# Pair bias with 8 stationary weights in four column strips, x loaded ahead of the pair, group statistics in whole-array steps

## The chip, the cores and the metric

The kernel runs on one core of one Trainium2 chip, with all data in 32-bit floating point. The metric is the device time of one execution in microseconds (us). PE is the matmul engine, PEld its loads of stationary weights, DVE the vector engine, ACT the scalar engine, POOL the GpSimd engine, and SP the engine whose queue issues most of the DMA transfers.

## The reference, cut to what matters

x has 128 rows s of 256 positions and 256 channels. Two layers follow one another, each of the form x + attention(groupnorm(x)), with 32 groups of 8 channels whose mean and variance are taken over all rows and positions.

```python
# layer 0: 8 heads of 32 channels
bias = einsum('nijz,zh->nhij', pair_repr, bias_proj)      # pair_repr: 256 x 256 x 128, bias_proj: 128 x 8
gate = sigmoid(xn @ gate_proj)
q, k, v = split(xn @ qkv_proj, 3)
sim = softmax(q k^T / sqrt(32)) + bias                    # the bias comes after the softmax
x = x + ((sim v) * gate) @ out_proj
# layer 1: 4 heads of 64 channels, keys within 16 positions of the query
q, k, v = split(xn @ w_in.T + b_in, 3)
x = x + softmax(mask(q k^T / sqrt(64))) v @ w_out.T + b_out
```

## The kernel before, in words

The program is written with named tiles in pools. A scheduler keeps each engine's instructions close to the written order and puts in the waits; a tile of a pool with n buffers is written again only when the use n tiles before is over. PSUM is shared by three pools: two banks for projections (`proj_bank`, taken in turn by everything that asks), four for scores (`sim_bank`), and one each of `avz` and `bv0`.

**Pair stage.** Eight chunks of x (32 positions per partition, `x_chunk`, L148) are loaded and their statistics taken with 32 `bn_stats` (L153), one per group. Sixteen chunks of the pair (`pair_chunk`, L181), each 32 values of i by 128 of j, go into a bias table `bias_sb` with j on the partitions. A chunk is transposed on PE four blocks at a time (L192), copied out of PSUM by ACT (L194), and then every transposed block of 128x128 is loaded as the stationary operand and multiplied with the 8 columns of `bias_w_sb` (L197). A last copy (L202) puts heads and i in order. The loop takes one chunk of x and one of the pair by turns (L207), so SP's queue has their loads (L151, L184) by turns, two buffers for each. After the loop `group_columns` (L110) makes mean and 1/std per channel: 32 `bn_aggr` on DVE (L113), then two small matmuls over partitions (L117, L130), a square root on ACT (L139) and a reciprocal (L141).

**Layer 0.** Each row s has two half steps, one per four heads. A half step makes scores of its four heads (L311), then some projections (in half 0: q and k of the next row and the transposes px of the row after; in half 1: v and the gate of the next row, and the output projection po of the row before), then `attend` for the half step before. The projections take the two proj banks in the fixed order q, k, px, v, gate, po. ACT makes the exponentials `ex` (L318) and copies q, k and v; DVE adds the two key tiles of `ex` (`both`, L321), since the denominator is a matmul of ones with that sum (L349). `attend` multiplies `ex` and the bias table with v in four column strips (L336, L343), and then:

```python
nc.scalar.activation(z, avz[:, 1, :], AF.Identity, accum_out=zsum[:, n : n + 1])   # L354
nc.vector.tensor_tensor(t, bv0, z, ALU.mult)                                       # L356
nc.vector.tensor_tensor(t, avz[:, 0, :], t, ALU.add)                               # L357
nc.vector.scalar_tensor_tensor(d, st[s]["e"][:, half, :], 1.0, z, ...)             # L359
nc.vector.reciprocal(d, d)                                                         # L360
nc.vector.tensor_tensor(st[s]["at"][:, half, :], t, d, ALU.mult)                   # L363
nc.vector.tensor_reduce(zmin[:, n : n + 1], z, axis=AX.X, op=ALU.min)              # L364
```

`finish` (L366) adds x to po (L374); every eighth row it stores the block and takes its statistics with 32 `bn_stats` (L379). After the last row `group_columns` runs again for layer 1, and the first loads of layer 1 (L414) wait for its last instruction.

**Layer 1** has one step per row, with masked exponentials multiplied on POOL (L455), z copied with its sum (L479), a reciprocal of 512 columns (L481), `at` (L483), the minimum (L485), and additions on DVE (L435, L495) and POOL (L496).

The minima and sums of z serve a test at the end (L519 to L530): if a denominator was outside a range of safe values, both layers are computed again with shifted exponentials. With these inputs that part isn't entered.

Of the kernel before, what the change touches and what calls it, by code (L numbers as in the profile page):

```python
# [9 lines left out]
F32 = mybir.dt.float32  # L10
AF = mybir.ActivationFunctionType
ALU = mybir.AluOpType
# [19 lines left out]
def conv_preact_kernel(  # L32
# [37 lines left out]
    eps = const.tile([P, 1], F32, name="eps")  # L70
    nc.gpsimd.memset(eps, EPS)

    bias_w_sb = const.tile([P, H0], F32, name="bias_w_sb")
    nc.scalar.dma_start(out=bias_w_sb, in_=bias_w)
    qkv_sb = const.tile([P, 2, 3 * C], F32, name="qkv_sb")
    nc.scalar.dma_start(out=qkv_sb, in_=qkv_w.rearrange("(t p) o -> p t o", p=P))
    gate_sb = const.tile([P, 2, C], F32, name="gate_sb")
# [29 lines left out]
    zsum = const.tile([P, 3 * S], F32, name="zsum")  # L107


    def group_columns(pool, stats, which):  # L110
        mv = pool.tile([P, G, 2], F32, name=f"mv{which}")
        for g in range(G):
            nc.vector.bn_aggr(out=mv[:, g, :], in_=stats[:, g, :, :].rearrange("p n s -> p (n s)"))  # L113
        means = pool.tile([P, G], F32, name=f"means{which}")
        nc.vector.tensor_copy(means, mv[:, :, 0])
        ps_m = proj_bank(f"ps_m{which}")
        nc.tensor.matmul(ps_m[:, 0, 0:G], lhsT=avg, rhs=means, start=True, stop=True)  # L117
        d = pool.tile([P, G], F32, name=f"d{which}")
        nc.vector.tensor_tensor(d, means, ps_m[:, 0, 0:G], ALU.subtract)
        v = pool.tile([P, G], F32, name=f"v{which}")  # L120
        nc.vector.tensor_tensor(v, d, d, ALU.mult)
        nc.vector.tensor_tensor(v, v, mv[:, :, 1], ALU.add)
        wide = pool.tile([P, 2, G, CG], F32, name=f"wide{which}")
        nc.vector.tensor_copy(wide[:, 0], means.unsqueeze(2).to_broadcast([P, G, CG]))
        nc.vector.tensor_copy(wide[:, 1], v.unsqueeze(2).to_broadcast([P, G, CG]))
        flat = wide.rearrange("p k g c -> p k (g c)")
        ps_c = proj_bank(f"ps_c{which}")
        for k in range(2):
            for half in range(2):
                nc.tensor.matmul(  # L130
                    ps_c[:, 0, 2 * k + half : 2 * k + half + 1],
                    lhsT=flat[:, k, half * P : (half + 1) * P],
                    rhs=avg[:, 0:1],
                    start=True, stop=True,
                )
        mean = const.tile([P, 2], F32, name=f"mean{which}")
        nc.vector.tensor_copy(mean, ps_c[:, 0, 0:2])
        std = pool.tile([P, 2], F32, name=f"std{which}")
        nc.scalar.activation(std, ps_c[:, 0, 2:4], AF.Sqrt, bias=eps)  # L139
        rstd = const.tile([P, 2], F32, name=f"rstd{which}")  # L140
        nc.vector.reciprocal(rstd, std)  # L141
        return mean, rstd
# [12 lines left out]

    with ExitStack() as early:
        xs_pool = early.enter_context(tc.tile_pool(name="xs", bufs=2))
        pr_pool = early.enter_context(tc.tile_pool(name="pr", bufs=2))
        st_pool = early.enter_context(tc.tile_pool(name="st", bufs=1))

        w_nat = st_pool.tile([P, 8, C], F32, name="w_nat")
        nc.scalar.dma_start(out=w_nat[:, 0:6, :], in_=w_in.rearrange("(t p) c -> p t c", p=P))
        nc.scalar.dma_start(out=w_nat[:, 6:8, :], in_=w_out.rearrange("(t p) c -> p t c", p=P))
        for o4 in range(2):
            for kt in range(2):
                pw = proj_bank(f"pw{o4}_{kt}").rearrange("p a b -> p (a b)")
                for j in range(4):
                    nc.tensor.transpose(
                        pw[:, j * P : (j + 1) * P], w_nat[:, 4 * o4 + j, kt * P : (kt + 1) * P], ident
                    )  # L170
                if o4 == 0:
                    nc.scalar.copy(w_in_t[:, kt, 0:512], pw)
                else:
                    nc.scalar.copy(w_in_t[:, kt, 512:768], pw[:, 0:256])
                    nc.scalar.copy(w_out_t[:, kt, :], pw[:, 256:512])

        stats = st_pool.tile([P, G, NX, 6], F32, name="stats0")
        IC = 32
        NPR = 2 * (R // IC)

        def pair_chunk(n):  # L181
            kt, ic = divmod(n, R // IC)
            pr = pr_pool.tile([P, IC, Z], F32, tag="pr", name=f"pr{n}")
            nc.sync.dma_start(  # L184
                out=pr,
                in_=pair[0, ic * IC : (ic + 1) * IC, kt * P : (kt + 1) * P, :].rearrange("i j z -> j i z"),
            )
            pb = proj_bank(f"pb{n}").rearrange("p a b -> p (a b)")
            for i4 in range(IC // 4):
                pz = sim_bank(f"pz{n}_{i4}").rearrange("p a b -> p (a b)")  # L190
                for i in range(4):
                    nc.tensor.transpose(pz[:, i * P : (i + 1) * P], pr[:, 4 * i4 + i, :], ident)  # L192
                prt = pr_pool.tile([P, 512], F32, tag="prt", name=f"prt{n}_{i4}", bufs=3)
                nc.scalar.copy(prt, pz)  # L194
                for i in range(4):
                    ii = 4 * i4 + i
                    nc.tensor.matmul(  # L197
                        pb[:, ii * H0 : (ii + 1) * H0],
                        lhsT=prt[:, i * P : (i + 1) * P], rhs=bias_w_sb,
                        start=True, stop=True,  # L200
                    )
            nc.scalar.copy(  # L202
                bias_sb[:, kt, :, ic * IC : (ic + 1) * IC],
                pb[:, 0 : IC * H0].rearrange("p (i h) -> p h i", h=H0),
            )

        for n in range(max(NX, NPR)):  # L207
            if n < NX:
                x_chunk(xs_pool, stats, x[0], n, "0_")
            if n < NPR:  # L210
                pair_chunk(n)
        mean0, rstd0 = group_columns(st_pool, stats, 0)


    XG = min(4, S)
# [40 lines left out]
    def rows(ap, s0, n):  # L256
        return ap[s0 : s0 + n].rearrange("s (t p) c -> p s t c", p=P)

    x1 = dram.tile([S, R, C], F32, name="x1")
    SG = min(8, S)  # L260

# [4 lines left out]
    with ExitStack() as lay:  # L266
        st1 = lay.enter_context(tc.tile_pool(name="st1", bufs=1))
        stats1 = st1.tile([P, G, S // SG, 6], F32, name="stats1")
        with ExitStack() as lay0:
# [11 lines left out]
            def piece(s, n):  # L281
# [6 lines left out]
                elif n in (1, 2):  # L288
                    w = "qk"[n - 1]
                    ps = by_channel(qkv_sb, (n - 1) * C, st[s]["xn"], f"p{w}{s}")  # L290
                    a = row.tile([P, 2, R], F32, tag=w, name=f"{w}{s}")
                    nc.scalar.copy(a, ps)
                    st[s][w] = a
                elif n == 3:
                    ps = by_token(st[s]["xn"], qkv_sb, 2 * C, f"pv{s}")
                    v = row.tile([P, 2, C], F32, tag="v", name=f"v{s}", bufs=3)
                    nc.scalar.copy(v, ps)
                    st[s]["v"] = v
                elif n == 4:
                    ps = by_channel(gate_sb, 0, st[s]["xn"], f"pg{s}")  # L300
                    e = row.tile([P, 2, R], F32, tag="e", name=f"e{s}", bufs=3)
                    nc.scalar.activation(e, ps, AF.Exp, scale=-1.0)
                    st[s]["e"] = e

            def scores(s, half):
# [11 lines left out]
                for j in range(4):  # L317
                    nc.scalar.activation(ex[:, j], sims[j], AF.Exp, scale=1.0 / math.sqrt(D0))  # L318
                both = att.tile([P, 4, R], F32, tag="both", name=f"both{s}_{half}")
                for j in range(0, 4, 2):  # L320
                    nc.vector.tensor_tensor(both[:, j : j + 2], ex[:, j : j + 2, 0, :], ex[:, j : j + 2, 1, :], ALU.add)  # L321
                hd[s, half] = (ex, both)

            def attend(s, half):
# [25 lines left out]
                        avz[ps, 1, :], lhsT=ones[:, 0:D0], rhs=both[:, j, :], start=True, stop=True  # L350
                    )
                z = att.tile([P, R], F32, tag="z", name=f"z{s}_{half}")
                n = 2 * s + half
                nc.scalar.activation(z, avz[:, 1, :], AF.Identity, accum_out=zsum[:, n : n + 1])  # L354
                t = att.tile([P, R], F32, tag="t", name=f"t{s}_{half}")
                nc.vector.tensor_tensor(t, bv0, z, ALU.mult)  # L356
                nc.vector.tensor_tensor(t, avz[:, 0, :], t, ALU.add)  # L357
# [3 lines left out]
                if half == 0:  # L361
                    st[s]["at"] = row.tile([P, 2, R], F32, tag="at", name=f"at{s}")
                nc.vector.tensor_tensor(st[s]["at"][:, half, :], t, d, ALU.mult)  # L363
                nc.vector.tensor_reduce(zmin[:, n : n + 1], z, axis=AX.X, op=ALU.min)  # L364

            def finish(s):  # L366
                if s < 0:
# [20 lines left out]
            for i in range(n_steps + 2):  # L388
# [10 lines left out]
                    finish(s - 1)  # L399
                if 0 <= i - 1 < n_steps:  # L400
                    attend(*divmod(i - 1, 2))
        mean1, rstd1 = group_columns(st1, stats1, 1)


    with ExitStack() as lay:
# [55 lines left out]
        def attend(s):  # L461
# [13 lines left out]
                                start=(kt == 0), stop=(kt == 1), skip_group_check=True,  # L475
                            )
            z = att.tile([P, 2, R], F32, tag="z", name=f"1z{s}")
            n = 2 * S + s
            nc.scalar.activation(z, zs, AF.Identity, accum_out=zsum[:, n : n + 1])  # L479
            rz = att.tile([P, 2, R], F32, tag="rz", name=f"1rz{s}")  # L480
            nc.vector.reciprocal(rz, z)  # L481
            at = row.tile([P, 2, R], F32, tag="at", name=f"1at{s}")
            nc.vector.tensor_tensor(at, av, rz, ALU.mult)  # L483
            st[s]["at"] = at
            nc.vector.tensor_reduce(zmin[:, n : n + 1], z, axis=AX.XY, op=ALU.min)  # L485

        def finish(s):
            if s < 0:
# [41 lines left out]
    with tc.If(sure < P):  # L530
        with ExitStack() as lay:
# [103 lines left out]
                again(0, s, x[0], x1, mean0, rstd0)  # L635
            for n in range(NX):
                x_chunk(two, stats2, x1, n, "2_")
            mean2, rstd2 = group_columns(one, stats2, 2)
            with tc.For_i(0, S, 1) as s:
                again(1, s, x1, out[0], mean2, rstd2)  # L640

# [24 lines left out]
```

## Time and profile before

| what | us |
|---|---|
| median of the 3 runs (3970.82 to 3972.38) | 3971.9 |
| the profiled execution, its own time | 3971.9 |
| its span, first to last instruction | 3970.1 |
| first transposes of the pair | 29.25 |
| first load of layer 0's rows issued | 348.3 |
| first transposes of layer 0 (px) | 354.3 |
| last addition of layer 0 (L374) | 2458.9 |
| first transposes of layer 1 | 2489.6 |

Busy shares of the span: PE 98%, PEld 77%, DVE 62%, ACT 37%, POOL 13%; mean granted PE clock 0.951.

How to read the profile: the page cuts the span into 40 slices of 99 us, one digit per slice, the busy share in tenths, and "PEclk" the share of the full clock that PE was granted. In the timeline a line has the start, the time in us from the first start to the last end of like instructions that follow each other, the engine, the line, the tiles as output<-inputs, shapes, the number of instructions and in brackets the idle time before with what ended it. A matmul of 32-bit data is two records. The records of matmuls overlap, so a PE that is busy all the time isn't a PE at its peak; where it matters the distance from one start to the next is given. In a group a line ends with the busy time of all, the mean duration of one in ns, and the idle time before.

### The profile page before, as it was taken

Reading aid. Unit: us, or ns where it says so; the run is one execution under the profiler, and the core shown is the slowest. Engines: PE = TensorE matmul, PEld = TensorE weight load, DVE = VectorE, ACT = ScalarE, POOL = GpSimd, SP = SyncE. Lnnn points to the kernel's source line nnn. Section 1 sums busy time; section 2 is a strip of 40 time slices with the busy share of each in tenths; the row PEclk is TensorE's granted clock in tenths of the full one; section 3 lists DMA queues with packets and bytes.
Section 4 is the critical chain, followed back from the end, with each engine's and each line's share of the span. In section 5 each row is a group of like instructions: output and inputs, shape, how many; then the busy total and the mean of one; then the engine's idle time right before and its main releaser. Section 6 shows DMA issues by size and latency. Waiting matters only on the chain. (4 is left out here: it accounts for less than half of the span.)

```text
span 3970.1 us, 75105 instructions
## 1 busy us (share of the span) xinstructions
PE 3877.4 (98%) x32294; PEld 3057.5 (77%) x32294; DVE 2457.1 (62%) x4181; ACT 1487.1 (37%) x3485; POOL 501.2 (13%) x270
## 2 busy tenths in 40 slices
PE   7999999999999999999999997999999999999998
PEld 7998777777777777777777774788888888888887
DVE  5402677767776777677766777456556555555655
ACT  2223444444444444444444442333333333333332
POOL 0000000000000000000000000233333333333333
PEclk6556999999999999999999998999999999999999
DMA  9631011101110111001110100111111111111111
GB/s 360 217 106 54 12 44 33 44 12 44 33 44 12 44 35 42 26 30 44 33 41 15 44 23 22 54 43 43 53 55 43 43 43 43 60 48 43 43 43 33
DMA packets 153826, 208.83 MB, mean 53 GB/s; under 512 B 2960, under 2 KB 135824, under 8 KB 152464
## 3 DMA queue, kind: packets, MB, share of 16 engines
q1 hardware_dynamic: 150656, 201.34, 15.8%
q8 instruction: 256, 4.19, 0.4%
q10 hardware_dynamic: 2832, 2.63, 0.2%
q14 instruction: 82, 0.67, 0.1%
HBM read 136.85 MB, written 67.11 MB: 51 GB/s over the span
## 5 line engine op out<-in xcount | busy, mean ns | idle before, releaser
L455 POOL TENSOR_TENSOR 1p<-1ex,seen 128x1152 f32<-128x1152 f32 x128 | 336.0, 2625 | 2758.9 <-ACT 1ex L453 2758.9
L481 DVE RECIPROCAL 1rz<-1z 128x512 f32<-128x512 f32 x128 | 429.2, 3353 | 246.9 <-ACT 1z L479 246.9
L318 ACT ACTIVATE ex<-sim 128x512 f32<-128x512 f32 x1024 | 528.7, 602 | 129.0 <-PE sim L311 129.0
L360 DVE RECIPROCAL d<-d 128x256 f32<-128x256 f32 x256 | 445.9, 1742 | 0.0
L356 DVE TENSOR_TENSOR t<-bv,z 128x256 f32<-128x256 f32 x256 | 108.1, 422 | 460.2 <-ACT z L354 460.2
L354 ACT ACTIVATE z<-avz 128x256 f32<-128x256 f32 x256 | 98.3, 384 | 750.4 <-PE avz L349 739.2
L479 ACT ACTIVATE 1z<-1zs 128x512 f32<-128x512 f32 x128 | 76.4, 597 | 729.0 <-issue 719.8
L321 DVE TENSOR_TENSOR both<-ex 128x512 f32<-128x512 f32 x512 | 329.1, 683 | 2.9 <-ACT ex L318 2.9
L311 PE MATMUL sim<-q,k 32*128 32x256 f32 x4096 | 293.3, 400 | 0.0
L336 PE MATMUL avz<-ex,v 128*32 128x256 f32 x4096 | 275.6, 386 | 10.5 <-DVE t L357 10.5
L343 PE MATMUL bv<-bias_sb,v 128*32 128x256 f32 x4096 | 269.6, 379 | 1.1 <-DVE t L356 1.1
L311 PEld LDWEIGHTS sim<-q,k 32*128 32x128 f32 x4096 | 184.9, 184 | 110.5 <-issue 104.9
L227 DVE TENSOR_SCALAR xn<-px,mean,rstd 128x256 f32<-128x256 f32 x512 | 253.8, 537 | 23.8 <-PE px L222 21.3
L250 PE MATMUL 1po<-w_out_t,1at 128*128 128x256 f32 x1024 | 256.9, 394 | 0.8 <-DVE 1at L483 0.8
L239 PE MATMUL p1q<-xn,w_in_t 128*128 128x256 f32 x1024 | 257.0, 394 | 0.6 <-DVE xn L227 0.6
L239 PE MATMUL pq<-xn,qkv_sb 128*128 128x256 f32 x1024 | 256.7, 394 | 0.8 <-DVE xn L227 0.7
L250 PE MATMUL pv<-qkv_sb,xn 128*128 128x256 f32 x1024 | 255.1, 392 | 0.0
L250 PE MATMUL po<-out_sb,at 128*128 128x256 f32 x1024 | 247.5, 382 | 6.5 <-DVE at L363 4.9
L496 POOL TENSOR_TENSOR 1o<-1o,yg 128x512 f32<-128x512 f32 x128 | 162.9, 1273 | 701.8 <-DVE 1o L495 699.2
L239 PE MATMUL p1k<-xn,w_in_t 128*128 128x256 f32 x1024 | 242.4, 380 | 0.0
L239 PE MATMUL pg<-xn,gate_sb 128*128 128x256 f32 x1024 | 241.9, 379 | 0.0
L250 PE MATMUL p1v<-w_in_t,xn 128*128 128x256 f32 x1024 | 241.9, 379 | 0.0
(91 smaller groups left out, 6314.6 us busy)
## 6 DMA issues: line engine op xcount, KB each, us to landing
xs<-in_x_dram SPq DMA_DIRECT2D x8, 4096.0 KB, 22.1
xg<-in_x_dram SPq DMA_DIRECT2D x32, 1024.0 KB, 7.5
x<-o SPq DMA_DIRECT2D x16, 2048.0 KB, 8.4
yg<-x SPq DMA_DIRECT2D x32, 1024.0 KB, 8.1
out_dram<-1o SPq DMA_DIRECT2D x32, 1024.0 KB, 5.3
qkv_sb<-in_L_conv_qkv_proj_dram ACTq DMA_DIRECT2D x1, 768.0 KB, 13.7
w_nat<-in_L_conv_w_in_dram ACTq DMA_DIRECT2D x1, 768.0 KB, 8.0
gate_sb<-in_L_conv_gate_proj_dram ACTq DMA_DIRECT2D x1, 256.0 KB, 14.0
```

The source lines that it names most:

```text
L227: nc.vector.tensor_scalar(xn[:, half, :], px[:, half, :], mean[:, half : half + 1], rstd[:, half : half + 1], op0=ALU.subtract, op1=ALU.mult,)
L239: nc.tensor.matmul(ps[:, m, :], lhsT=w[:, kt, col + m * P : col + (m + 1) * P], rhs=xn[:, kt, :], start=(kt == 0), stop=(kt == 1),)
L250: nc.tensor.matmul(ps[:, t, :], lhsT=a[:, kt, t * P : (t + 1) * P], rhs=w[:, kt, col : col + C], start=(kt == 0), stop=(kt == 1),)
L311: nc.tensor.matmul(sims[j][:, kt, :], lhsT=k[p0 : p0 + D0, half, kt * P : (kt + 1) * P], rhs=q[p0 : p0 + D0, half, :], start=True, stop=True,)
L318: nc.scalar.activation(ex[:, j], sims[j], AF.Exp, scale=1.0 / math.sqrt(D0))
L321: nc.vector.tensor_tensor(both[:, j : j + 2], ex[:, j : j + 2, 0, :], ex[:, j : j + 2, 1, :], ALU.add)
L336: nc.tensor.matmul(avz[ps, 0, :], lhsT=v[:, kt, ch], rhs=ex[:, j, kt, :], start=(kt == 0), stop=(kt == 1),)
L343: nc.tensor.matmul(bv0[ps, :], lhsT=v[:, kt, ch], rhs=bias_sb[:, kt, 4 * half + j, :], start=(kt == 0), stop=(kt == 1),)
L360: nc.vector.reciprocal(d, d)
L455: nc.gpsimd.tensor_tensor(p, ex.rearrange("p h k q -> p h (k q)"), seen.rearrange("p k q -> p (k q)").unsqueeze(1).to_broadcast([P, H1, 2 ...
L481: nc.vector.reciprocal(rz, z)
L496: nc.gpsimd.tensor_tensor(o[:, k], o[:, k], xgs[g][:, k], ALU.add)
```

## The change

The diff, without its context. Line numbers after the change are some 25 higher in the layers.

- The pair's product is turned round. The 8 columns of `bias_w_sb`, padded with zeros to 32, are the stationary operand, in four column strips; a transposed group of 4 blocks (512 columns) is the moving one. The result has heads on the partitions, so it is copied out (`bs`) and transposed back, and DVE puts it into the table with four small copies for every 16 values of i. Of the copies of transposed groups out of PSUM every other one goes to DVE. The pair has three buffers instead of two, transposed groups eight instead of three.
- All loads and statistics of x are written ahead of the pair's chunks, and so is layer 0's `group_columns`.
- `group_columns` has reductions over all groups at once in place of 32 `bn_aggr`.
- In layer 0 the sum of the two key tiles is one POOL instruction instead of two on DVE; v is copied by DVE instead of ACT.
- In both layers z is copied without its sum, and a second reduction on DVE (`watch`) makes the sum.

```diff
-    bias_w_sb = const.tile([P, H0], F32, name="bias_w_sb")
-    nc.scalar.dma_start(out=bias_w_sb, in_=bias_w)
+    bias_w_sb = const.tile([P, 32], F32, name="bias_w_sb")
+    nc.gpsimd.memset(bias_w_sb, 0.0)
+    nc.scalar.dma_start(out=bias_w_sb[:, 0:H0], in_=bias_w)
...
-    def group_columns(pool, stats, which):
-        mv = pool.tile([P, G, 2], F32, name=f"mv{which}")
-        for g in range(G):
-            nc.vector.bn_aggr(out=mv[:, g, :], in_=stats[:, g, :, :].rearrange("p n s -> p (n s)"))
+    def group_columns(pool, stats, count, which):
+        tri = stats.rearrange("p g n (e k) -> p g (n e) k", k=3)
+        n = tri.shape[2]
         means = pool.tile([P, G], F32, name=f"means{which}")
-        nc.vector.tensor_copy(means, mv[:, :, 0])
+        nc.vector.tensor_reduce(means, tri[:, :, :, 1], axis=AX.X, op=ALU.add)
+        nc.vector.tensor_scalar(means, means, 1.0 / n, None, op0=ALU.mult)
+        dev = pool.tile([P, G, n], F32, name=f"dev{which}")
+        nc.vector.tensor_tensor(dev, tri[:, :, :, 1], means.unsqueeze(2).to_broadcast([P, G, n]), ALU.subtract)
+        nc.vector.tensor_tensor(dev, dev, dev, ALU.mult)
+        nc.vector.scalar_tensor_tensor(
+            dev, tri[:, :, :, 2], 1.0 / count, dev, op0=ALU.mult, op1=ALU.add
+        )
+        within = pool.tile([P, G], F32, name=f"within{which}")
+        nc.vector.tensor_reduce(within, dev, axis=AX.X, op=ALU.add)
...
-        nc.vector.tensor_tensor(v, v, mv[:, :, 1], ALU.add)
+        nc.vector.scalar_tensor_tensor(v, within, 1.0 / n, v, op0=ALU.mult, op1=ALU.add)
...
-        pr_pool = early.enter_context(tc.tile_pool(name="pr", bufs=2))
+        pr_pool = early.enter_context(tc.tile_pool(name="pr", bufs=3))
...
-            pb = proj_bank(f"pb{n}").rearrange("p a b -> p (a b)")
-            for i4 in range(IC // 4):
-                pz = sim_bank(f"pz{n}_{i4}").rearrange("p a b -> p (a b)")
+            for part in range(IC // 16):
+                prts = []
+                for g in range(4):
+                    pz = sim_bank(f"pz{n}_{part}_{g}").rearrange("p a b -> p (a b)")
+                    for i in range(4):
+                        nc.tensor.transpose(pz[:, i * P : (i + 1) * P], pr[:, 16 * part + 4 * g + i, :], ident)
+                    prt = pr_pool.tile([P, 512], F32, tag="prt", name=f"prt{n}_{part}_{g}", bufs=8)
+                    if g % 2 == 0:
+                        nc.scalar.copy(prt, pz)
+                    else:
+                        nc.vector.tensor_copy(prt, pz)
+                    prts.append(prt)
+                pb = proj_bank(f"pb{n}_{part}").rearrange("p a b -> p (a b)")
+                for g in range(4):
+                    nc.tensor.matmul(
+                        pb[32 * g : 32 * (g + 1), :], lhsT=bias_w_sb, rhs=prts[g], start=True, stop=True
+                    )
+                bs = pr_pool.tile([P, 4, P], F32, tag="bs", name=f"bs{n}_{part}", bufs=2)
+                nc.scalar.copy(bs.rearrange("p i j -> p (i j)"), pb)
+                pt = ps_av.tile([P, 4, 4, 32], F32, tag="avz", name=f"pbt{n}_{part}")
                 for i in range(4):
-                    nc.tensor.transpose(pz[:, i * P : (i + 1) * P], pr[:, 4 * i4 + i, :], ident)
-                prt = pr_pool.tile([P, 512], F32, tag="prt", name=f"prt{n}_{i4}", bufs=3)
-                nc.scalar.copy(prt, pz)
+                    nc.tensor.transpose(pt[:, i].rearrange("p g h -> p (g h)"), bs[:, i, :], ident)
+                i0 = ic * IC + 16 * part
                 for i in range(4):
-                    ii = 4 * i4 + i
-                    nc.tensor.matmul(
-                        pb[:, ii * H0 : (ii + 1) * H0],
-                        lhsT=prt[:, i * P : (i + 1) * P], rhs=bias_w_sb,
-                        start=True, stop=True,
-                    )
-            nc.scalar.copy(
-                bias_sb[:, kt, :, ic * IC : (ic + 1) * IC],
-                pb[:, 0 : IC * H0].rearrange("p (i h) -> p h i", h=H0),
-            )
-        for n in range(max(NX, NPR)):
-            if n < NX:
-                x_chunk(xs_pool, stats, x[0], n, "0_")
-            if n < NPR:
-                pair_chunk(n)
-        mean0, rstd0 = group_columns(st_pool, stats, 0)
+                    nc.vector.tensor_copy(
+                        bias_sb[:, kt, :, i0 + i : i0 + 16 : 4], pt[:, i, :, 0:H0].rearrange("p g h -> p h g")
+                    )
+        for n in range(NX):
+            x_chunk(xs_pool, stats, x[0], n, "0_")
+        mean0, rstd0 = group_columns(st_pool, stats, TCH * CG // 2, 0)
+        for n in range(NPR):
+            pair_chunk(n)
...
+    def watch(z, n):
+        nc.vector.tensor_reduce(zmin[:, n : n + 1], z, axis=AX.X, op=ALU.min)
+        nc.vector.tensor_reduce(zsum[:, n : n + 1], z, axis=AX.X, op=ALU.add)
...
-                    nc.scalar.copy(v, ps)
+                    nc.vector.tensor_copy(v, ps)
...
-                for j in range(0, 4, 2):
-                    nc.vector.tensor_tensor(both[:, j : j + 2], ex[:, j : j + 2, 0, :], ex[:, j : j + 2, 1, :], ALU.add)
+                nc.gpsimd.tensor_tensor(both, ex[:, :, 0, :], ex[:, :, 1, :], ALU.add)
...
-                n = 2 * s + half
-                nc.scalar.activation(z, avz[:, 1, :], AF.Identity, accum_out=zsum[:, n : n + 1])
+                nc.scalar.copy(z, avz[:, 1, :])
...
-                nc.vector.tensor_reduce(zmin[:, n : n + 1], z, axis=AX.X, op=ALU.min)
+                watch(z, 2 * s + half)
...
-            n = 2 * S + s
-            nc.scalar.activation(z, zs, AF.Identity, accum_out=zsum[:, n : n + 1])
+            nc.scalar.copy(z, zs)
...
-            nc.vector.tensor_reduce(zmin[:, n : n + 1], z, axis=AX.XY, op=ALU.min)
+            watch(z.rearrange("p a b -> p (a b)"), 2 * S + s)
```

## The prediction

> **What bounds the kernel now.** I read the slices of the page first, then stretches of the span by stage, then the groups of instructions and the waits of the first stage, last the timeline of one row. The slices: TensorE (PE) is busy everywhere, but in the first four of 40 slices its granted clock is about half, and the DMA is full only there.
>
> ```profile
> PE   7999999999999999999999997999999999999998
> PEclk6556999999999999999999998999999999999999
> DMA  9631011101110111001110100111111111111111
> ```
>
> The stretches (us; busy us per engine; then clock, DMA share, GB/s) say the same in numbers: the pair stage runs at clock 0.50 with VectorE (DVE) idle, layer 0 at 1.00 with PE busy 99%.
>
> ```profile
> 200.00:250.00 50.00, 50.00 (x244) 50.00 (x244) 0.00 (x0) 12.86 (x23) 0.00 (x0) 0.50 0.37 103
> 600.00:1000.00 400.00, 397.80 (x3821) 287.90 (x3820) 281.50 (x562) 175.97 (x391) 0.00 (x0) 1.00 0.10 33
> ```
>
> The groups show what fills the pair stage: 1024 matmuls of 8 columns, each with its own load of 128x128 weights, and 512 transposes; and SP's own waits show that pair loads wait for PE, not the reverse.
>
> ```profile
> L197 PEld LDWEIGHTS pb<-bias_w_sb,prt 128*128 128x128 f32 x1024 | 232.1, 333 | 2.2 <-ACT prt L194 2.2
> L197 PE MATMUL pb<-bias_w_sb,prt 128*128 128x8 f32 x1024 | 220.9, 347 | 0.0
> L192 PEld LDWEIGHTS pz<-ident,pr 128*128 128x128 f32 x512 | 114.7, 259 | 4.5 <-DMA pr<-in_L_conv_pair_repr_dram 4.5
> SPq L184 <- PE pz L192: 209.6, 14, 19.1
> ```
>
> In single records both kinds start 213 ns apart; a chunk takes 19.7 us (pr issues 264.91, 284.64, 304.38), 16 of them from 29.25 to 348. Layers 0 and 1 are PE too: half steps of 8.75 and 7.46 us, row after row, 11.41 us a row in layer 1.
>
> **What the Trainium skill says.** "TensorE: Matmul & The Clock Gate", Part 1: the array has half clock by default and full clock after some 3.4 us of sustained activity. The clock records agree: full for 3.4 us from 24.6 us, right after the 16 transposes pw, half from 28.0 to 359.1, full 3 us after pq begins. Same page, "LDWEIGHTS (loading the stationary operand)": a load is paid by its columns; here a 32-column load (L343) takes 110 ns, a 128-column one (L250) 190. "TensorEngine Tiling (Array Packing)", "Key Properties": tiles run in parallel and a change of mode drains the array; the four strips of L336 start 7 ns apart and each four take 213 ns, with a gap of 0.2 to 0.3 us when the mode changes. "VectorE: DVE Perf Modes", "Mode 2×_2P": PSUM has one read port for DVE, so a 32-bit copy out of it runs one element per cycle; the trace has no wide copy from PSUM on DVE, but L374, with one PSUM operand, takes 691 ns for 512.
>
> **The change, part by part.** The profiled execution has 3971.9 us (span 3970.1, 1.8 around it), the median of the runs, so the sum is made against it.
>
> *Loads of x first.* SP now issues eight xs, then sixteen pr. The first xs lands at 13.06; the second is issued near 15, behind a lane that the weights' loads use (as L184 is now, 15.08). The bias weights' load now waits for a POOL memset and goes out behind w_nat: some 1 us in a queue that nothing else waits for. One xs streams 10.85 us (records 1.84 to 12.69), its 32 bn_stats take 10.55, two buffers: 11.4 us a chunk with 1 us of issue each second time, so the eighth lands at 30 + 6 x 11.4 = 98.4 and DVE is through at 110. PE idles from 25 to 106 where it now begins at 29: that costs 77 us of start.
>
> *Pair chunks.* Per 16 rows PE has 16 transposes x 110 ns (px, full clock) = 1.76, eight records of 512 columns: by L336 213 x 2 per four = 0.85, four transposes back 0.44, mode changes 0.4: 3.45, so 6.9 us a chunk. DMA: a lone pr streams in 7.73 us (207.19 to 214.92); its 64 packets of 116 ns per engine are 7.43. I take 7.5 (a PE that loses over 0.3 us a part to waits for copies would set the pace instead: at 7.9 a chunk +6): DMA ends last, from 98.4 to 218.4. ACT has 3 copies x 587 = 1.76, DVE two of 0.69 and four small ones between 0.19 (L119, 128x32) and 0.3: 2.1 to 2.6 of 3.75, hidden. After the last landing: two parts of PE 6.9 and the last copies 1: 227. Then the xg load, 348.32 to 354.26 now, 6 us: layer 0 begins at 233 instead of 354.3: **-121**. The statistics of layer 0 (with their Sqrt table load, 1.28 on ACT) move under the pair's loads: nothing, and little if uncovered.
>
> *Statistics between the layers.* This lies bare on the path:
>
> ```profile
> 2459.67 6.28 DVE L379 BATCH_NORM_STATS2 stats<-o 128x6 f32<-128x128 f32 x32
> 2465.86 14.43 DVE L113 BATCH_NORM_AGGREGATE mv<-stats 128x2 f32<-128x96 f32 x32
> 2480.32 0.18 DVE L115 COPY means<-mv 128x32 f32<-128x32 f32 x1
> ...
> 2483.98 2.65 SPq L414 DMA_DIRECT2D yg<-x  x3
> ```
>
> 14.6 us go; two reductions of 1024 (L485: 0.63 for 512, 1.04 ns an element: 1.16), three passes (L435: 0.69 for 512: 1.23) and a small one come, 6.2: **-8.4**. Strided reads could halve the gain.
>
> *Sums of key tiles on POOL.* 512 x 683 ns leave DVE. One add of 1024: between L455 and L496 2.11 ns an element, 2.35 (2.55 at L496's rate). Its result is read a half step later; the exponentials of the half step of 1005 end at 1008.31, and the matmuls that read their sum come after the next scores, at 1020.75: 12 us of room. Nothing, unless an add took over 8 us. Room on DVE was not on PE's path except once in 8 rows, where 32 bn_stats make PE lose 0.69 at avz and 0.38 at po: 15 times 1.07.
>
> *Copy of v on DVE.* This one is on PE's path. The line before po in one row:
>
> ```profile
> 1007.99 1.89 PE L239 MATMUL pg<-xn,gate_sb 128*128 128x256 f32 x8
> 1008.19 0.60 ACT L297 COPY v<-pv 128x512 f32<-128x512 f32 x1
> 1008.45 0.36 DVE L364 TENSOR_REDUCE zmin<-z 128x1 f32<-128x256 f32 x1
> 1008.73 0.41 DVE L363 TENSOR_TENSOR at<-t,d 128x256 f32<-128x256 f32 x1
> 1009.05 1.28 DVE L321 TENSOR_TENSOR both<-ex 128x512 f32<-128x512 f32 x2
> 1009.72 1.89 PE L250 MATMUL po<-out_sb,at 128*128 128x256 f32 x8
> ```
>
> po takes the projection bank that pv leaves (two banks in turn), so it now waits for DVE instead of ACT. DVE's order in the changed program is zmin, at, zsum, v, o. Its chain starts 0.09 earlier, since the accumulator read (194 ns) after z is gone: zsum at 8.95, v at 9.23 to 9.92 with 0.69; po's weights can load at 9.96 (as at 1043.53, 46 ns after at). A po that restarts has its second matmul 0.32 after its load; undelayed that is at 9.934 - 0.32 = 9.61. So PE loses 0.35 in each of 112 rows; in the 16 with bn_stats po loses 0.80 in place of 0.38. **+39 +7 = +46.** Were the copy at two elements per cycle (0.42), 0.07 a row, +9. Behind po nothing else queues that isn't PE.
>
> *zsum and z elsewhere.* In layer 0 zsum is 0.28 in that chain. In layer 1 it fills 0.63 of the 1.30 us in which DVE waits for p1v: nothing.
>
> Sum: 3971.9 - 121 - 8.4 + 46 = 3888.5; with 1.5 us for slips at the stage's start, **3890**.
>
> **Rivals.**
> 1. *The copy of v does not stall PE* (shorter, or the chain starts earlier): +0 to +9 in place of +46: 3850. For it: an edge of 0.35 us. Against: both durations are from rows.
> 2. *The clock drops again.* PE then waits for DMA, and and PE idles part of each chunk (6.9 of 7.5 us in use). Now and then at half clock, a chunk takes 9 us: 16 x 1.5 = +24, with a longer tail 3918. Half clock throughout: 20 x 213 + 1.7 + 0.3 = 6.2 a part, 12.4 a chunk, 106 + 198 + 9 = 313, -41 -8 +46: 3969, no change. For it: the mix of today, four transposes in twelve loads and the rest of 8 columns, never leaves half clock in 319 us; against: the 16 transposes pw in a row raised it, and pb's 512 columns stream longer than they load.
> 3. *Slower: POOL's add and DVE share SBUF, and DVE's chain ahead of po stretches.* The chain from z to v is 4.24 us, and each us more is a us of PE per row. It decides from 0.98 us a row (126/128), and doubled DVE times under a 2.35 us add give 1.5 more: +192 on 3890, 4082. Against: in layer 1 zmin (627 for 512) runs beside POOL's 1p at the rate that L364 (360 for 256) has without.
>
> **How the numbers follow.** The forecast 0.60 (own range 3872 to 3912), rival 1 0.17, a clock now and then low 0.10, low throughout 0.06 (of it 0.04 within 0.2%), slower by rival 3 0.06, with 0.01 for slips within 0.2%. About 0.2%, 8 us, is what a measurement can tell from no change. Faster 0.60 + 0.17 + 0.10 + 0.02 = 0.89, same 0.05, slower 0.06. The range 3840 to 3945 leaves out rival 3, the low clock throughout and the ends of the others, under 2 in 10.
>
> **What would show it.** Right: clock near 1.0 from about 110 us, pr landing every 7.5 us, PE waiting for DMA pr there; px at 233; group sums of 6 us between the layers; PE po waiting for DVE v and half steps of 9.1 and 7.46. Wrong: clock 0.5 and chunks of 12 us (rival 2), half steps of 8.75 (rival 1), DVE rows longer than now beside POOL (rival 3).

## The result, and the profile after

| | median us | range, runs | to the kernel before, 95% interval |
|---|---|---|---|
| before | 3971.9 | 3970.8 to 3972.4, 4 | 1 |
| after | 4373.4 | 4372.5 to 4377.6, 4 | 1.101, 1.099 to 1.103 |

The forecast was 3890, range 3840 to 3945. The change made the kernel 10% slower: the sign is wrong, and the time lies far outside the range. By stages, from the starts of PE's first instruction of each:

| stretch | before | after | difference | forecast |
|---|---|---|---|---|
| start to the first px of layer 0 | 354.3 | 264.7 | -89.6 | -121 |
| layer 0 and the way to layer 1's first px | 2135.3 | 2626.3 | +491.0 | +37.6 |
| layer 1 to the end | 1480.5 | 1481.1 | +0.6 | 0 |

The slices of the page after, as they were shown of before:

```profile
PE   0988888888888888888888888879999999999998
PEclk9999999999999999999999999989999999999999
DMA  9620100100100100000001000011111111111110
```

The first slice has DMA and no PE, as forecast; the second, PE at full clock. The new thing is layer 0: from slice 3 to 26 PE is an 8, where it was a 9. The stretches (busy us of PE, PEld, DVE, ACT, POOL; then clock, DMA share, GB/s):

```profile
200.00:250.00 50.00, 50.00 (x300) 28.28 (x300) 18.06 (x65) 18.10 (x32) 0.00 (x0) 1.00 0.50 169
600.00:1000.00 400.00, 351.52 (x3052) 241.97 (x3052) 284.14 (x450) 128.31 (x256) 92.42 (x40) 0.93 0.09 30
```

The pair stage has clock 1.00 where it had 0.50. In layer 0 PE is idle 12% of the time and its clock is 0.93 where it was 1.00: 3052 records in 400 us, not 3821. The half steps say where: the first of each row takes 7.459 us (median) as before, the second 12.62 on average instead of 8.78 (127 of them: +487 us). The groups of layer 0 show what grew:

```profile
L346 POOL TENSOR_TENSOR both<-ex 128x1024 f32<-128x1024 f32 x256 | 601.7, 2350 | 2247.3 <-ACT ex L344 2247.3
L387 DVE TENSOR_TENSOR at<-t,d 128x256 f32<-128x256 f32 x256 | 599.6, 2342 | 0.0
L323 DVE COPY v<-pv 128x512 f32<-128x512 f32 x128 | 86.4, 675 | 8.9 <-PE pv L271 8.9
L283 DVE TENSOR_REDUCE zsum<-z 128x1 f32<-128x256 f32 x256 | 103.8, 405 | 0.0
```

The POOL add takes 2350 ns (2.35 us had been forecast), the copy of v 675 ns (0.69), zsum 405. But `at`, a product of 256 columns that the change doesn't touch, has gone from 407 to 2342 ns. And PE waits for v, nearly once a row:

```profile
PE po L271 <- DVE v L323: 282.5, 126, 2.5
```

The timeline of one row:

```profile
1512.33 2.06 ACT L344 ACTIVATE ex<-sim 128x512 f32<-128x512 f32 x4 [0.67 <-PE sim L337]
1512.70 1.74 DVE L384 RECIPROCAL d<-d 128x256 f32<-128x256 f32 x1
1514.01 1.89 PE L260 MATMUL pg<-xn,gate_sb 128*128 128x256 f32 x8
1514.36 0.36 DVE L282 TENSOR_REDUCE zmin<-z 128x1 f32<-128x256 f32 x1
1514.54 2.35 POOL L346 TENSOR_TENSOR both<-ex 128x1024 f32<-128x1024 f32 x1 [5.10 <-ACT ex L344]
1514.64 2.53 DVE L387 TENSOR_TENSOR at<-t,d 128x256 f32<-128x256 f32 x1
1517.09 0.41 DVE L283 TENSOR_REDUCE zsum<-z 128x1 f32<-128x256 f32 x1
1517.42 0.67 DVE L323 COPY v<-pv 128x512 f32<-128x512 f32 x1
1518.14 2.63 PE L271 MATMUL po<-out_sb,at 128*128 128x256 f32 x8 [2.24 <-DVE v L323]
```

The exponentials end at 1514.39; POOL begins its add 0.15 later, and `at` begins 0.10 after that. It ends at 1517.17, 0.28 after the add: it has stood still as long as the add ran. zsum and v queue behind it, and po, which could have loaded at 1515.5, loads at 1518.14. zmin, with one operand in SBUF, runs into the add and keeps its 0.36. The `at` of the first half step is held as well (over 1 us in 111 of its 128 cases, and in 126 of the 128 of the second), but no matmul waits for it there, since po comes in the second half step: the first one keeps its 7.459 us.

### The profile page after: what moved, and what is told of

Read it like the earlier page. It is cut to its first block, busy times and chain, and to the rows that moved or that the text cites. A ratio compares the mean times of both kernels' runs of the same rounds, so it can differ in the third digit from the quotient of the medians.

```text
span 4372.1 us, 73931 instructions
## 1 busy us (share of the span) xinstructions
PE 3917.0 (90%) x31654; PEld 2901.2 (66%) x31654; DVE 2931.0 (67%) x4319; ACT 1358.2 (31%) x2925; POOL 1103.0 (25%) x527
## 5 line engine op out<-in xcount | busy, mean ns | idle before, releaser
L346 POOL TENSOR_TENSOR both<-ex 128x1024 f32<-128x1024 f32 x256 | 601.7, 2350 | 2247.3 <-ACT ex L344 2247.3
L271 PE MATMUL po<-out_sb,at 128*128 128x256 f32 x1024 | 388.7, 546 | 288.7 <-DVE v L323 282.5
L387 DVE TENSOR_TENSOR at<-t,d 128x256 f32<-128x256 f32 x256 | 599.6, 2342 | 0.0
L271 PEld LDWEIGHTS po<-out_sb,at 128*128 128x128 f32 x1024 | 257.2, 262 | 388.3 <-DVE v L323 333.1
L378 ACT COPY z<-avz 128x256 f32<-128x256 f32 x256 | 95.2, 372 | 1249.2 <-PE avz L374 1239.1
L398 DVE TENSOR_TENSOR o<-po,xg 128x512 f32<-128x512 f32 x128 | 88.5, 691 | 398.6 <-PE po L271 398.6
L361 PE MATMUL avz<-ex,v 128*32 128x256 f32 x4096 | 317.6, 433 | 19.8 <-DVE t L381 18.4
L502 ACT COPY 1z<-1zs 128x512 f32<-128x512 f32 x128 | 75.0, 586 | 729.1 <-issue 720.0
```

The costliest lines, as they stand in the source:

```text
L271: nc.tensor.matmul(ps[:, t, :], lhsT=a[:, kt, t * P : (t + 1) * P], rhs=w[:, kt, col : col + C], start=(kt == 0), stop=(kt == 1),)
L346: nc.gpsimd.tensor_tensor(both, ex[:, :, 0, :], ex[:, :, 1, :], ALU.add)
L361: nc.tensor.matmul(avz[ps, 0, :], lhsT=v[:, kt, ch], rhs=ex[:, j, kt, :], start=(kt == 0), stop=(kt == 1),)
```

## The experiments

**Theory 1**: a POOL add holds SBUF, and a DVE instruction with both operands in SBUF waits for its end; po waits behind. The Trainium skill says so, on a page that the prediction did not use: "SBUF — State Buffer", section "SBUF: two separate sides". POOL and DVE share a pair of ports by an exclusive lock, not by splitting bandwidth; a DVE instruction with two SBUF inputs takes part in it against a POOL instruction that reads SBUF, and whichever starts first has it for the whole instruction. **Theory 2**: the place of v's copy, on DVE behind the chain, is the cost. **Theory 3**: the add slows whatever DVE does beside it, by sharing bandwidth. A second question is what the lower clock is worth, a third why the pair stage gained 31 us less than forecast. Ratios have the 95% interval in brackets.

### Undoing one part

**e1**: the sums back on DVE, behind v.

```diff
-                nc.gpsimd.tensor_tensor(both, ex[:, :, 0, :], ex[:, :, 1, :], ALU.add)
...
+            def sums(s, half):
+                ex, both = hd[s, half]
+                for j in range(0, 4, 2):
+                    nc.vector.tensor_tensor(both[:, j : j + 2], ex[:, j : j + 2, 0, :], ex[:, j : j + 2, 1, :], ALU.add)
...
+                        with tc.issue_after(st[s + 1]["vi"]):
+                            sums(s, half)
```

> The changed kernel with the sums of the key tiles back on DVE (two adds of 512 per half step, issued behind the copy of v, so that v keeps its place); v stays on DVE. Theory 1 (the POOL add holds SBUF while DVE's product at waits, and po waits behind it): at<-t,d falls from 2342 ns to about 410, half step B from 12.6 to about 9.1 us, and the time is 3972 - 90 (pair stage) - 5 (statistics) + 46 (v) = about 3925. Theory 2 (the copy of v on DVE alone makes po late and drops the clock): half step B stays near 12.6 and the time near 4370.

Measured: 3945.8, ratio 0.9935 (0.9915 to 0.9955). `at` 413 ns, the second half step 9.14 us, clock in the span 0.993. Theory 2 falls: v is where the change put it, and the time is 428 us lower. The 20 us above the expectation lie in the 15 rows whose half step follows the `bn_stats`: 10.81 us, where the kernel before has 9.13. In each of these rows PE waits once for 1.79 to 2.01 us, and the clock stays at 1.00.

**e2**: only v back on ACT (`nc.scalar.copy(v, ps)` in place of `nc.vector.tensor_copy(v, ps)`).

> The changed kernel with only the copy of v back on ACT; the sum stays on POOL. Theory 1: at still takes about 2.3 us and now po waits for at itself, which ended at 17.17 in the row looked at where po could have loaded at 15.52: a stall of about 1.7 us instead of 2.6, so at least 0.97 us a row less, 4250; if the shorter stall also spares the clock, down to about 4080. Theory 2: at no longer matters, half step B is 8.75 and the time about 3880.

Measured: 4025.1, ratio 1.013 (1.011 to 1.016). `at` still takes 2343 ns; half steps of 9.90 us, 1.15 over the 8.75 of before; clock 1.00 between 400 and 2300 us. So the held `at` alone costs 1.15 us a row, and that wait does not bring the clock down. The time is below both figures of Theory 1 (4250 and 4080): two of po's eight records run while `at` is held, and PE waits 0.91 us a row, where 1.7 had been expected.

**e4**: both undone, all else as changed.

> The changed kernel with the sums and the copy of v both where they were (DVE and ACT); pair stage, statistics and zsum as changed. All theories: half step B 8.75 to 9.0 us, layer 0 at clock 1.00, the pair stage's 90 us and 5 us of the statistics kept: about 3878, 0.976 of the kernel before. Above 3890 the changes that are left cost something in layer 0.

Measured: 3881.3, ratio 0.977 (0.976 to 0.979), half step 8.75. This is the rest of the change: 90 us gained.

**e11**: the reverse, the kernel before with only the POOL line.

> The kernel before with one line changed: the sums of the key tiles on POOL. at starts near 8.7 in the row shown and the exponentials end at 8.3, so at waits for the add as in e2_v_act: half step B 8.75 + 1.15 = 9.90, the time 3972 + 127 x 1.15 = about 4118. If z's accumulator read shifts the chain enough to let at go first, the add waits instead and the time stays at 3972.

Measured: 4118.3, ratio 1.037 (1.035 to 1.039); half steps of 9.90. One line costs 146 us by itself. In eight of the 256 half steps the second case of the expectation came: `at` began first, 0.07 to 0.14 us ahead of the add. It then kept its 0.41 us, and the add took 2.48 to 2.56 us instead of 2.35. Four of the eight are second half steps of a row; they took 8.75 us, as in the kernel before. One of them:

```profile
1105.98 0.41 DVE L362 TENSOR_TENSOR at<-t,d 128x256 f32<-128x256 f32 x1
1106.08 2.52 POOL L320 TENSOR_TENSOR both<-ex 128x1024 f32<-128x1024 f32 x1 [5.42 <-ACT ex L318]
1106.97 1.89 PE L250 MATMUL po<-out_sb,at 128*128 128x256 f32 x8
```

### Is it a lock, and on what

**e3**: the add stays on POOL, v on DVE; only one operand of `at` moves, from SBUF to PSUM.

```diff
-                bv0 = ps_av.tile([P, R], F32, tag="bv0", name=f"bv0{s}_{half}")
+                bv2 = ps_av.tile([P, 2, R], F32, tag="bv0", name=f"bv0{s}_{half}")
+                bv0 = bv2[:, 0, :]
...
-                nc.vector.reciprocal(d, d)
+                nc.vector.reciprocal(bv2[:, 1, :], d)
...
-                nc.vector.tensor_tensor(st[s]["at"][:, half, :], t, d, ALU.mult)
+                nc.vector.tensor_tensor(st[s]["at"][:, half, :], t, bv2[:, 1, :], ALU.mult)
```

> The changed kernel, but the reciprocal is written to the unused half of the PSUM bank of bv, so that the product at reads one operand from SBUF and one from PSUM. POOL keeps its add, v stays on DVE. Theory 1, in the form that DVE stops for POOL only where both of its operands are in SBUF: at is about 0.4 to 0.5 us beside the running add, half step B about 9.1 and the time about 3925. Theory 3 (the add slows whatever DVE does beside it, by sharing bandwidth): at stays above 1 us and half step B above 11, the time above 4150.

Measured: 3962.6, ratio 0.998 (0.997 to 0.999). The two groups of this run:

```profile
L346 POOL TENSOR_TENSOR both<-ex 128x1024 f32<-128x1024 f32 x256 | 603.3, 2357 | 1836.9 <-ACT ex L344 1836.9
L388 DVE TENSOR_TENSOR at<-t,bv 128x256 f32<-128x256 f32 x256 | 103.8, 406 | 0.0
```

And one row of its timeline, where the add and `at` begin in the same order and 0.10 us apart as in the row above:

```profile
1351.87 2.35 POOL L346 TENSOR_TENSOR both<-ex 128x1024 f32<-128x1024 f32 x1 [5.10 <-ACT ex L344]
1351.97 0.41 DVE L388 TENSOR_TENSOR at<-t,bv 128x256 f32<-128x256 f32 x1
1352.29 0.41 DVE L283 TENSOR_REDUCE zsum<-z 128x1 f32<-128x256 f32 x1
```

406 ns beside a running add, and 2342 with the same operand in SBUF. Theory 3 falls: what decides is that both operands are in SBUF. The changed kernel agrees: in 15 half steps behind `bn_stats` `t` (one operand in PSUM) began beside a running add and took 407 ns, and `d` (both in SBUF), just behind it, was held until 0.28 us after the add's end. The half step is 9.14, as in e1. That the time is 38 us above the expectation has another cause, in the 15 rows with `bn_stats`: `d` (two SBUF operands) comes late there, meets the add, and PE then waits for the PSUM bank that this edit keeps until `at` is read (first half steps of 10.1 us where they were 8.1; in nine of the 15 the clock drops after the two waits, and they are 11.0 to 11.4).

**e9**: operands and engines of e2, and only the moment of the add changed, by a POOL copy of one element that reads `at`.

```diff
+                if s > 0:
+                    nc.gpsimd.tensor_copy(both[:, 0, 0:1], st[s - 1]["at"][:, half, 0:1])
                 nc.gpsimd.tensor_tensor(both, ex[:, :, 0, :], ex[:, :, 1, :], ALU.add)
```

> The run with v back on ACT and the sum on POOL (e2_v_act, 4025), with one POOL copy of one element per partition ahead of each add, which reads the at that DVE forms in the same half step: the add starts some 0.5 us later, when at is done, and nothing else changes. Theory 1 (the add holds DVE because it starts 0.1 us before at): at takes 0.41 us, half step B 8.75, the time 3881 or a few us less, since DVE is 1.3 us a half step freer in the rows with bn_stats. Theory 3 (the add slows what DVE does beside it): zsum, o and the next chain get longer instead, and the time stays above 3950.

Measured: 3880.5, ratio 0.977 (0.975 to 0.979), against 1.013 for e2: 145 us for an add that starts 0.9 us later. One row of it:

```profile
1004.55 0.41 DVE L389 TENSOR_TENSOR at<-t,d 128x256 f32<-128x256 f32 x1
1004.88 0.41 DVE L283 TENSOR_REDUCE zsum<-z 128x1 f32<-128x256 f32 x1
1005.09 0.18 POOL L347 COPY both<-at 128x1 f32<-128x1 f32 x1 [4.82 <-DVE at L389]
1005.36 2.35 POOL L348 TENSOR_TENSOR both<-ex 128x1024 f32<-128x1024 f32 x1
1005.44 1.70 PEld L271 LDWEIGHTS po<-out_sb,at 128*128 128x128 f32 x8
```

`at` is done before the add begins, and po loads in this row with no wait. The few microseconds hoped for beyond e4 did not come: behind the `bn_stats` the add meets `d`, which is held in 16 half steps (1.58 us, median).

**e12**: the changed kernel whole, v on DVE, with that one copy.

> The changed kernel, whole, with only the one-element POOL copy of at ahead of each add (as in e9_sum_after_at). at 0.41 us, then zsum and v: half step B 9.14 as in e1_sum_dve, and in the rows with bn_stats below the 10.8 of that run, since the sums are not on DVE: 3881 + 0.39 x 110 + at most 0.4 x 15 = about 3930. If the rows with bn_stats stay at 10.8: 3945.

Measured: 3945.5, ratio 0.993 (0.992 to 0.995). One tiny instruction takes back 428 us. The rows with `bn_stats` stay at 10.75 us, the upper case; there the whole DVE chain is late after the `bn_stats`, so that the add, which waits for the late `at`, runs into `d` of the next half step:

```profile
430.46 2.36 POOL L348 TENSOR_TENSOR both<-ex 128x1024 f32<-128x1024 f32 x1
...
431.55 1.55 DVE L385 SCALAR_TENSOR_TENSOR d<-e,z 128x256 f32<-128x256 f32 x1
433.03 0.41 DVE L383 TENSOR_TENSOR t<-avz,t 128x256 f32<-128x256 f32 x1
```

`d` takes 1.55 us instead of 0.42 and ends 0.28 after the add, as `at` did: the same hold on another instruction.

### What the lower clock is worth

**e6**: the changed kernel, with five matmuls per row in PE's queue ahead of po whose result nothing reads.

```diff
+                fill[0] = bv2
...
+                for j in range(5):
+                    nc.tensor.matmul(fill[0][:, 1, :], lhsT=ident, rhs=bias_sb[:, 0, j % H0, :], start=True, stop=True)
                 po = by_token(st[s]["at"], out_sb, 0, f"po{s}")
```

> The changed kernel with five extra matmuls per row (256 columns each, into the unused half of bv's PSUM bank, read by nobody) in PE's queue ahead of po, some 2.4 us, so that PE works while it would wait for v. Theory 1 with its second part (the wait of 2.5 us makes the throttle grant half clock for a window): clock in layer 0 back to 1.00, half step B 11.26 instead of 12.6 mean, the time 4373 - 127 x 1.4 to 1.6 = about 4180. If the lower clock is no part of the loss, or the extra work is paid in full: 4370 or above.

Measured: 4197.0, ratio 1.057 (1.054 to 1.059): 176 us less, by more work.

```profile
600.00:1000.00 400.00, 395.52 (x3515) 288.74 (x3508) 302.53 (x450) 139.60 (x277) 100.21 (x43) 1.00 0.08 25
```

`at` still takes 2354 ns and the second half step is 11.24 us on average (11.27 in nearly every row): the wait is there, filled, and the clock is 1.00. In the changed kernel the clock records of layer 0 have 108 stretches of 3.41 us at half clock, 368.6 us; half of that, 184, is lost work, which agrees with the 176.

### The pair stage

**e7**: e4 with PE's order in the pair stage fixed by ordering edges: `first` makes the 16 transposes of part p, `back` the four transposes back of part p - 2, `second` the four products of part p - 1.

```diff
+        def in_order(block):
+
+            if done:
+                with tc.issue_after(done[-1]):
+                    last = block()
...
+            done.append(last.ins)
...
+                in_order(first)
...
+                in_order(lambda: back(bss.pop(p - 2), mt, mc * IC + 16 * k, f"{m}_{k}"))
...
+                in_order(second)
```

> The run with both moves of layer 0 undone (e4_both_back, 3881), with PE's order in the pair stage fixed: 16 transposes of a part, then the four transposes back of the part before last, then the four products of the part before, so that no product waits for a copy. If what lengthened a part from 3.45 to 4.65 us is the split products with their changes of mode and waits for copies: 3.2 to 3.5 us a part, the stage 32 x 1.2 = 38 us shorter, the time about 3843. If a part is set by the copies on ACT and DVE or by the loads: no more than 10 us shorter, 3871 or above.

Measured: 3845.2, ratio 0.968 (0.966 to 0.970): 36 us below e4, as the first case had it. One part and the start of the next:

```profile
151.89 1.97 PE L208 MATMUL pz<-ident,pr 128*128 128x128 f32 x16
...
153.69 0.60 PE L230 MATMUL pbt<-ident,bsq 128*128 128x128 f32 x4
...
154.22 1.06 PE L220 MATMUL pbq<-prt,bias_w_sb 128*32 128x512 f32 x8
...
155.22 0.33 PE L208 MATMUL pz<-ident,pr 128*128 128x128 f32 x1
```

3.33 us from start to start (1.80 + 0.53 + 1.00), and the first px at 228.4. In the changed kernel a part took 4.7 on average (104.2 to 255.2 for 32) and 4.95 near 150 us: in 19 of the 32 parts the scheduler put transposes of the next part between the products of three strips and that of the fourth, for which a copy was late; in the other 13 the four stand together, but spread out, since they too wait for their copies. Four products together cost 1.00 up to the next transpose; split three and one they cost 1.34 + 0.98, since each group streams its two passes alone and 0.52 us pass from its last start to the next transpose. e7 takes away both, the splits and the waits for copies, and does not tell them apart.

**e8**: as e7, with two pair loads behind each load of x, and the copies of the stage on ACT.

> As e7_pair_order, with two pair loads behind each load of x as they were issued in turn before, all copies of the pair stage on ACT (DVE has the statistics), and the group statistics after both. Bound by the loads: 8 x (10.85 + 2 x 5.5) + 13 = 188, layer 0 begins at about 201 instead of 264, the time about 3817. If the clock falls to half since PE works only 3.3 of 5.5 us of each part, a part takes about 6.2 us: layer 0 begins near 225, the time about 3840. If ACT's copies set the pace (3.7 us a part), still 201.

Measured: 3821.2, ratio 0.962 (0.961 to 0.964), first px at 204.6, where the loads alone had been reckoned at 201. The loads bind, and not ACT's copies: DMA is busy all the time from 20 to 180 us (395 GB/s between 50 and 100), ACT 55% of it. The clock there was 0.83: rival 2 of the prediction, here, and hidden by the loads.

**e10**: e8 with the sum of z on ACT in layer 0, as it was.

> e8_pair_between (3821) with the sum of z back on ACT in layer 0, as an accumulation of the copy z, as before the change. zsum on DVE makes the rows with bn_stats 9.456 long where they had 9.152: 15 x 0.30 = 4.6 us less, about 3817. If the chain starts later by the accumulator read and that counts in every row: 3821 or more.

Measured: 3815.2 (3813.7 to 3817.4, 5 runs), ratio 0.961 (0.960 to 0.962); half steps behind `bn_stats` 9.13 again, where e8 has 9.45. It is the fastest version here, 156 us below the kernel before.

## Why the prediction was wrong, step by step

**"Sums of key tiles on POOL ... Nothing, unless an add took over 8 us": this step failed.** The add's price (2.35) and its 12 us of room were right. What was left out is that the add and `at` meet: the exponentials of a half step end just when the DVE chain of the half step before the last comes to `at`. The step looked for who waits for the add's result, and not for who works while it runs.

**Rival 3 had the mechanism's place and price and was set aside by a bad argument.** It said that POOL's add and DVE share SBUF and that each us in DVE's chain is a us of PE. Set against it was that layer 1's zmin runs beside a POOL product at its old rate. That observation is true and proves nothing: zmin has one operand in SBUF, and in the row above zmin runs undisturbed while `at` stands still. The trace of before held no case that could have shown the hold: in layer 1 only zmin, the reciprocal and 1at run beside POOL, and 1at has one of its operands (1av) in PSUM. Its form was wrong too: not doubled times, but a full stop to the add's end.

**The size of the loss** comes from waits in series. Against e4 (3881) the change costs 492: the add alone 144 (e2), v on DVE alone 65 (e1), the clock 176 (e6). What is left, 107 or 0.84 us a row, appears only with both moves. The traces suggest why, though no run separates the parts: zsum and v, 1.0 us, are exposed by 0.39 alone and wholly behind the held `at`; and the first two records of po, which in e2 run during the hold, must now wait for the bank that v leaves.

**Copy of v, +46: right mechanism, one term too small.** 0.35 a row was forecast, and e1 and e12 have 9.14 - 8.75 = 0.39. The term for the rows with `bn_stats`, 0.42 x 16 = 7, should have been about 1.3 x 15 = 20 (10.75 to 10.81 against the 9.46 of e4): DVE runs late there, and it has the sums to do as well (e1) or meets the POOL add (e12). Together 65.

**x first and pair chunks, -121: -90.** The eighth xs landed at 98.3 (98.4 forecast), PE began at 104.2 (106), the clock was 1.00 from 110 on, the tail with the xg load took 9.5 us from the last transpose. Two terms of the chunk were wrong. DMA does not need 7.5 us: with loads queued one landed every 5.5 us (103.4, 108.9, 114.4), since 7.73 was the time of a lone one. And 3.45 us a part, right for an order that keeps the four products together (e7: 3.33), was 4.7 in the order that the scheduler made; PE set the pace, and SP waited for it. PE's order is the scheduler's and not the diff's, and the step took the diff's.

**Statistics between the layers, -8.4: -8.1, in part by luck.** From the end of the last `bn_stats` to the first load of layer 1 (yg) 9.90 us pass, where 18.04 did:

```profile
2868.65 6.28 DVE L403 BATCH_NORM_STATS2 stats<-o 128x6 f32<-128x128 f32 x32
2874.96 1.50 DVE L117 TENSOR_REDUCE means<-stats 128x32 f32<-128x1024 f32 x1
2876.70 1.52 DVE L120 TENSOR_TENSOR dev<-stats,means 128x1024 f32<-128x1024 f32 x1
2878.26 1.22 DVE L121 TENSOR_TENSOR dev<-dev 128x1024 f32<-128x1024 f32 x1
2879.71 1.52 DVE L122 SCALAR_TENSOR_TENSOR dev<-stats,dev 128x1024 f32<-128x1024 f32 x1
2881.26 1.22 DVE L126 TENSOR_REDUCE within<-dev 128x32 f32<-128x1024 f32 x1
...
2884.82 2.65 SPq L438 DMA_DIRECT2D yg<-x  x3
```

The three passes that read `stats` with a stride take 1.50 to 1.52, the two on `dev` 1.22 as priced (1.16 and 1.23): 6.98 for the five where 6.01 was summed, and 7.55 with the small steps between them (6.2 forecast). But some of those small steps stood behind the `bn_aggr` before: after the last pass 2.34 us are left, where 3.69 followed. The forecast took this rest as unchanged, and the two errors nearly cancel.

**zsum, nothing:** right in layer 1 (+0.6 us over 128 rows). In layer 0 it costs 0.33 us in the 15 rows with `bn_stats`; e10 is 6.0 below e8.

**The range** left out rival 3, with a chance of 0.06, and so the case that came; rival 3's own price, 4082, was 291 too low, since neither the full stop nor the clock was in it.

## What to carry to other kernels

Before work is moved to POOL, list what DVE does at that moment: here an instruction with both operands in SBUF stopped until the POOL add ended, and one with an operand in PSUM (`at` in e3, `t`, the copy of v) or a reduction, a reciprocal or a `bn_stats` with a single operand in SBUF did not. A copy from SBUF to SBUF never met the add, so of that the runs show nothing. If they meet, move the moment (a one-element dependency was enough) or one operand. And where PE waits in every row, count the clock as well: here the wait was worth 316 us and the clock that it took away another 176.

## What the runs showed of the hardware that was not expected

- The hold is whole: `at` and `d` ended 0.28 us after the add, and over all 256 `at` the mean is 1.94 us longer. It goes both ways, as the Trainium skill has it ("SBUF — State Buffer", section "SBUF: two separate sides"): in e11 the add behind an `at` that had begun first took up to 0.2 us longer, and a tenth of a microsecond in the order of the two starts decided over 1.15 us of the row.
- One wait of PE of 2.24 us in some 20 us was enough for half clock (0.93 in layer 0). Single waits of 0.9 us (e2) and of 1.79 to 2.01 us (e1) were not, and two of 1.2 us within 3.5 us were in nine of fifteen rows (e3). The Trainium skill's page "TensorE: Matmul & The Clock Gate", section "Why this matters for your kernels", has gaps above some 3 us as the bound; here the measurement decides, and it is lower.
- In e7 the four column strips of the pair's product start 7 ns apart and stream together, 0.45 us from one pass of 512 columns to the next. The next transpose of 128 columns starts 0.52 us after the last start, 0.07 more than a further pass would.
